# The last periods of a staged kernel get orders of their own, and key-value products move one more token tile behind their keys

## The chip, the core and the metric

The kernel runs on one core of a Trainium2 chip. The metric is the device time of one execution in microseconds (us), taken as the median of several executions.

## What is computed

The input is 4 sequences of 2048 tokens with 256 channels, in float32. Four residual layers follow one another, each as `x = x + norm(layer(norm(x)))` with a plain layer norm over the 256 channels:

1. softmax attention with 16 heads of 16 channels; queries and keys are the normalised input, scaled per channel, and values are the normalised input itself;
2. a feed-forward layer with token shift: `r = sigmoid(W_r xr)`, `k = relu(W_k xk)^2`, output `r * (W_v k)`, where `xr` and `xk` mix each token with the one before it;
3. a linear-attention block: norm, `Q = elu(q)+1`, `K = elu(k)+1`, the sums `KV = sum K v` over the tokens of a whole sequence, the message `Q KV / (Q sum K)`, then a second norm and a GELU layer of 1024 hidden channels;
4. a gated layer with integer weights: `W_d (silu(W_g x) * (W_u x))` with 768 hidden channels.

## The kernel before

**Two parts.** `sandwich_kernel` first does layer 1 for all four sequences and writes the result to DRAM (`mids`). Then `rest` does layers 2 to 4. This change touches `rest` alone. `rest` is built twice, and a flag computed from the integer weights picks one at run time; these inputs take the branch `narrow`, in which the hidden values of layer 4 are split into a high part `gT` and a low part `gL`.

**Blocks, stages, periods.** `rest` works on 16 blocks of 512 tokens (4 token tiles of 128), 4 blocks to a sequence. A block passes four stages, written as Python generators: `stage_f` (layer 2), `stage_a` (first norms, queries, keys and values of layer 3), `stage_b` (message and GELU layer of layer 3) and `stage_i` (layer 4). In period `p`, stage f works on block `p`, stage a on `p - 2`, stage b on `p - 6` and stage i on `p - 7`. So f runs in periods 0 to 15, a in 2 to 17, b in 6 to 21, i in 7 to 22, and what is left of i in 23. From period 18 on only b and i are left.

**Order.** The strings `RAMP` (periods 0 to 5) and `FULL` (6 to 23) list the parts of the stages in the order in which one period issues them; `next:` and `last:` take a part of the neighbouring period's block. A part whose block does not exist is skipped. TensorE (PE), ScalarE (ACT) and VectorE (DVE) are wrapped in `InOrder`, which keeps their instructions in exactly this order; all of them carry the helper's line, L46, so the profile's rows are told apart by tile names. GpSimd (POOL) and the SyncE queue (SP) are not wrapped: a scheduler places their instructions as their inputs and their buffers allow, and each then runs its own list in order.

**Parts that matter here.**

- `b:pre` (POOL, L537): `hb <- x`, the layer norm applied to the four token tiles of the block. `next:b.pre` stands behind `b:down3` in `FULL`, and `hb` has one buffer.
- `b:msg`: per token tile two products `m <- kvm,QT` on PE, three DVE steps that end in `msg`, and a POOL add `hb <- hb,msg` (L310). `b:sums` are DVE statistics (`lnb`), and the root is taken on POOL (L533). `b:norm` is four ACT steps `h <- hb` behind two small POOL steps (L117, L118). `b:turn` is eight PE transposes `t <- ident,h` with two ACT evacuations into `zT`.
- `b:up0` to `b:up3`: two of the eight hidden tiles each, `m <- zT,w1T` on PE and GELU on ACT. `b:down0` to `b:down3`: one token tile each, `m <- w2T,hf` on PE, a DVE add `o <- m,b` and a POOL add `o <- o,hb` (L332).
- `b:osums`, `b:x`: statistics `lno` on DVE, root `lno_rs` on POOL, four DVE steps `o <- o,lno_mv,lno_rs`, four POOL adds `x <- x,o` (L140). `i:osums` and `i:x` are the same for stage i, with the output's DMA at the end; the freed buffer then takes the next block's load (`load`, pool `late`).
- `i:sums`, `i:norm`, `i:turn`: the same pattern with `lni`. Each `i:turn` evacuation is an ACT copy `hT` and a DVE difference `hL`, both from the PSUM tile `t`, of which there are two.
- `i:gate0` to `i:gate5`: eight PE products, SiLU on ACT, `gs <- m,gs` on DVE, the copy `gT` on ACT, `gL <- gs,gT` on POOL (L382). `i:down0` to `i:down3`: twelve PE products each from `gT` and `gL`, and an ACT copy `o <- m`.
- `a:kv0` to `a:kv3`: per token tile `m <- wkv,zT` on PE; then `elu` on DVE, the exponential on ACT, `K` on DVE and `v` on ACT. `gather` adds `kv <- v,K` on PE, one token tile behind. `a:kv4` does the last gather.

All products of `rest` write PSUM tiles `m`, of which there are four.

Of the kernel before, what the change touches and what calls it, by code (L numbers as in the profile page):

```python
# [10 lines left out]
FP = mybir.dt.float32  # L11
# [7 lines left out]
P = 128  # L19
C = 256  # L20
CC = C // P
# [28 lines left out]
def rest(ctx: ExitStack, tc: tile.TileContext, a: dict, out_rows, mids, env: dict, narrow: bool):  # L50
    nc = tc.nc
# [16 lines left out]
    NB = B * NBLK  # L68
    LAG_A, LAG_B, LAG_I = 2, 2 + NBLK, 3 + NBLK
    early = ctx.enter_context(tc.tile_pool(name="early", bufs=3))  # L70
    late = ctx.enter_context(tc.tile_pool(name="late", bufs=3))
    quer = ctx.enter_context(tc.tile_pool(name="quer", bufs=LAG_B - LAG_A + 1))
    small = ctx.enter_context(tc.tile_pool(name="small", bufs=LAG_B - LAG_A + 2))
    one = ctx.enter_context(tc.tile_pool(name="one", bufs=1))
    two = ctx.enter_context(tc.tile_pool(name="two", bufs=2))
    three = ctx.enter_context(tc.tile_pool(name="three", bufs=3))
# [7 lines left out]
        dve.tensor_scalar(wq[name], wi, 1.0 if narrow else DEQUANT, None, ALU.mult)  # L84

    kvms, vs = [], []
    for r in range(2):
        kvm = one.tile([P, CC, P + 4], FP, tag=f"kvm{r}", name=f"kvm{r}")
        nc.gpsimd.memset(kvm, 0.0)
        kvms.append(kvm)  # L90

        v = one.tile([P, CC, P + 4], FP, tag=f"v{r}", name=f"v{r}")
        nc.gpsimd.memset(v, 1.0 / T)
        vs.append(v)
# [12 lines left out]
    def sums(src, tag, pool=two):  # L107
        return ln_stats(pool, [src[:, i, :] for i in range(4)], tag, dve)
# [110 lines left out]
    def stage_a(j):  # L219
        x, k = xs[j], j % NBLK  # L220
        before[j] = st = sums(x, "lna", small)
        yield "sums"
        h = block_tile("h")
        norm(h, x, st)
        st = sums(h, "lnz")
        yield "norm"
        norm(h, h, st)
        yield "norm2"
        zT = three.tile([P, CC, IB], FP, tag="zT", name="zT")
        to_channels(h, affine(zT, g1, be1))  # L230
        yield "turn"
        queries[j] = QT = quer.tile([P, CC, IB], FP, tag="QT", name="QT")
        for d in range(CC):
            qp = mm_tile()
            linear(qp, lambda c: wqT[:, c, d * P : (d + 1) * P], lambda c: zT[:, c, :], CC)
            elu1(QT[:, d, :], qp, IB)
            yield f"q{d}"
        if k == 0:
            kvacc[0] = [ps_kv.tile([P, P + 4], FP, tag=f"kv{c}", name=f"kv{c}") for c in range(CC)]
        kv = kvacc[0]  # L240

        def gather(i, K, V):
            for c in range(CC):
                pe.matmul(
                    kv[c],
                    lhsT=K[:, c * P : (c + 1) * P],
                    rhs=V[:, c, :],
                    start=(k == 0 and i == 0),
                    stop=(k == NBLK - 1 and i == 3),
                )  # L250

        last = None
        for i in range(4):
            kvp = mm_tile()
            linear(kvp, lambda c: zT[:, c, i * P : (i + 1) * P], lambda c: wkv[:, c, :], CC)
            K = two.tile([P, C], FP, tag="K", name="K")
            elu1(K, kvp[:, :C], C)
            V = vs[i % 2]
            act.activation(
                V[:, :, :P],  # L260
                kvp[:, C:].rearrange("p (c d) -> p c d", c=CC),
                AF.Copy,
                scale=1.0 / T,
            )
            if last:
                gather(*last)
            last = i, K, V
            yield f"kv{i}"
        gather(*last)
        if k == NBLK - 1:  # L270
            kvm = kvms[j // NBLK % 2]
            for c in range(CC):
                for g in range(4):
                    rows = slice(32 * g, 32 * g + 32)
                    dve.tensor_copy(kvm[rows, c, rows], kv[c][rows, rows])
                    dve.tensor_copy(
                        kvm[rows, c, P + g : P + g + 1], kv[c][rows, P + g : P + g + 1]
                    )
        yield "kv4"


    def stage_b(j):
        x, kvm, QT = xs[j], kvms[j // NBLK % 2], queries.pop(j)
        mv, rs = before.pop(j)
        hb = one.tile([P, 4, C], FP, tag="hb", name="hb")
        for i in range(4):
            ln_apply(hb[:, i, :], x[:, i, :], mv, rs, i, nc.gpsimd)
        yield "pre"
        for i in range(4):
            mp = mm_tile()  # L290
            m3 = mp[:, : CC * (P + 4)].rearrange("p (c k) -> p c k", c=CC)
            for c in range(CC):
                pe.matmul(
                    m3[:, c, :],
                    lhsT=QT[:, c, i * P : (i + 1) * P],
                    rhs=kvm[:, c, :],
                    start=True,
                    stop=True,
                )
            zr = two.tile([P, CC, 4], FP, tag="zr", name="zr")  # L300
            dve.tensor_scalar(zr, m3[:, :, P : P + 4], EPS_ATTN / T, None, ALU.add)
            dve.reciprocal(zr, zr)
            msg = three.tile([P, C], FP, tag="msg", name="msg")
            dve.tensor_tensor(
                msg.rearrange("p (c h v) -> p c h v", c=CC, h=4),
                m3[:, :, :P].rearrange("p c (h v) -> p c h v", h=4),
                zr.unsqueeze(3).broadcast_to([P, CC, 4, 32]),
                ALU.mult,
            )
            nc.gpsimd.tensor_tensor(hb[:, i, :], hb[:, i, :], msg, ALU.add)  # L310
        yield "msg"
        st = sums(hb, "lnb")
        yield "sums"
        z = block_tile("h")
        norm(z, hb, st)
        yield "norm"
        zT = three.tile([P, CC, IB], FP, tag="zT", name="zT")
        to_channels(z, affine(zT, g2, be2))
        yield "turn"
        hf = one.tile([P, NF, IB], FP, tag="hf", name="hf")  # L320
        for f in range(NF):
            fp = mm_tile()
            linear(fp, lambda c: w1T[:, c, f * P : (f + 1) * P], lambda c: zT[:, c, :], CC)
            act.activation(hf[:, f, :], fp, AF.Gelu, bias=b1[:, f : f + 1])
            if f % 2:
                yield f"up{f // 2}"
        o = block_tile("o")
        for i in range(4):
            yp = mm_tile()
            linear(yp[:, :C], lambda f: hf[:, f, i * P : (i + 1) * P], lambda f: w2T[:, f, :], NF)  # L330
            dve.tensor_tensor(o[:, i, :], yp[:, :C], b2, ALU.add)
            nc.gpsimd.tensor_tensor(o[:, i, :], o[:, i, :], hb[:, i, :], ALU.add)  # L332
            yield f"down{i}"
        st = sums(o, "lno")
        yield "osums"
        apply(o, o, st)
        residual(x, o)
        yield "x"


    def stage_i(j):
# [67 lines left out]
    FULL = (  # L409
        "f:turn i:turn b:msg i:gate0 a:turn last:i.osums f:mix i:gate1 b:sums last:i.x load i:gate2 f:k0 "  # L410
# [4 lines left out]
    )  # L415
    RAMP = (
        "load f:turn a:turn f:mix a:q0 next:a.sums a:q1 f:k0 next:a.norm f:k1 a:kv0 next:f.sums a:kv1 "
        "next:a.norm2 a:kv2 next:f.norm a:kv3 f:r a:kv4 f:v f:osums f:x next:b.pre"
    )
    MAKE = {"f": (stage_f, 0), "a": (stage_a, LAG_A), "b": (stage_b, LAG_B), "i": (stage_i, LAG_I)}  # L420
    live = {}

    def step(p, stage, part):
        make, lag = MAKE[stage]
        j = p - lag
# [10 lines left out]
    for p in range(NB + LAG_I + 1):  # L436
        if p < 3:
            convert(("wgT", "wuT", "wdT")[p])
        for item in (RAMP if p < LAG_B else FULL).split():
            if item == "load":  # L440
                if p + 1 < NB:
                    load(p + 1, early)
                if 0 <= p + 1 - LAG_B < NB:
                    load(p + 1 - LAG_B, late)
                continue
            stage, part = item.split(":")
            at = p
            if stage in ("next", "last"):
                at = p + 1 if stage == "next" else p - 1
                stage, part = part.split(".")  # L450
            step(at, stage, part)
# [517 lines left out]
```

## Time and profile before

| | us |
|---|---|
| median of 3 runs | 4577.19 (4576.31 to 4578.02) |
| the profiled execution | 4576.01 |
| span of its instructions | 4574.2 |
| layer 1 (attention) | to about 3087 |
| periods 0 to 5 (`RAMP`) | to 3321 |
| periods 6 to 17 | 3321 to 4272.5 |
| periods 18 to 23 (b and i only) | 4272.5 to 4574.2 |

Period starts are read from the first transposes of `i:turn` (or `f:turn`) in the timeline. A row of the timeline has the start, the duration of all its instructions from first start to last end, the engine, the line, the operation, the tiles, the shape, the number of instructions, and in brackets the idle time before it and what ended it. A row of the windows has the stretch, its length, each engine's busy time with its instructions, the clock that TensorE was granted as a share of full speed, and the DMA share and rate. A row of the waits names the waiting engine and tile, what it waited for, the total, the number and the longest.

### The profile page before, as it was taken

The page shows a single profiled execution, that of the slowest core. Times are in us where ns is not written, and L with a number is a line of the kernel's source. Part 1 is how long each engine was busy: PE and PEld are TensorE (multiplying, and loading weights), DVE is VectorE, ACT ScalarE, POOL GpSimd, SP SyncE. Part 2 cuts the span into 40 slices and gives each one's busy share as a digit, 9 for nine tenths or more (in the row PEclk, how much of TensorE's full clock was granted, in tenths as well). Part 3 has the DMA queues.
Part 4 walks back from the last instruction along what each step waited for, and adds up shares of the span by engine and source line. Part 5 has one row for each costly group of instructions (what it writes and reads, how often), then busy time and mean ns, then how long its engine had stood idle before and what let it go on. Part 6 is the DMA issues. An engine that isn't in the chain of part 4 may idle for free.

```text
span 4574.2 us, 69494 instructions
## 1 busy us (share of the span) xinstructions
PE 4196.7 (92%) x26369; PEld 2196.9 (48%) x26369; DVE 3394.8 (74%) x6847; ACT 2874.5 (63%) x3558; POOL 1089.5 (24%) x1541
## 2 busy tenths in 40 slices
PE   4999999999999999999999999984789899899887
PEld 1444444444444444444444444432456666666665
DVE  4898898988889988889898888954555545554333
ACT  0677777777777777777777777763555555655343
POOL 3100111211001221011121100013234544444344
PEclk9999999999999999999999999997999999999998
DMA  3101101011010020110101101002000000000000
GB/s 107 38 10 29 29 10 42 29 43 36 11 30 23 25 65 10 29 29 10 43 29 31 38 10 29 1 24 72 33 14 28 19 33 24 28 19 19 10 19 15
DMA packets 84568, 130.58 MB, mean 29 GB/s; under 512 B 21376, under 2 KB 41984, under 8 KB 84224
## 3 DMA queue, kind: packets, MB, share of 16 engines
q1 hardware_dynamic: 77920, 122.23, 9.0%
q8 instruction: 210, 3.44, 0.3%
q10 hardware_dynamic: 6304, 3.81, 0.3%
q14 instruction: 134, 1.10, 0.1%
HBM read 33.70 MB, written 25.17 MB: 13 GB/s over the span
## 4 chain that ended last, share of the span: by engine, by line
PE 60%; DVE 21%; ACT 9%; POOL 5%; issue 4%; SPq 1%; DMA 1%; ACTq 0%; POOLq 0%; DVEq 0%
PE acc L46 19%; PE s L46 17%; PE w L46 13%; DVE mx L46 10%; PE m L46 8%; PE t L46 2%; ACT p L46 2%; DVE o L46 2%; ACT h L46 2%; POOL hb L537 2%; ACT L46 1%; DVE gs L46 1%; SPq L662 1%; ACT elu L46 1%; PE ot L46 1%
## 5 line engine op out<-in xcount | busy, mean ns | idle before, releaser
L46 DVE TENSOR_REDUCE mx<-s 128x1 f32<-128x512 f32 x4096 | 2538.8, 682 | 305.0 <-PE s L46 304.9
L46 ACT ACTIVATE p<-w 128x1024 f32<-128x1024 f32 x2048 | 2002.7, 1022 | 824.4 <-PE s L46 556.9
L46 PE MATMUL s<-k,q 64*128 64x512 f32 x4096 | 1664.3, 450 | 56.8 <-DMA k<-lo 30.3
L46 PE MATMUL w<-mrow,pick 64*128 64x512 f32 x4096 | 1406.2, 417 | 0.0
L46 PE MATMUL w<-q,k 64*128 64x512 f32 x4096 | 1369.3, 419 | 0.0
L46 PEld LDWEIGHTS s<-k,q 64*128 64x128 f32 x4096 | 758.5, 186 | 1269.2 <-DVE mx L46 1147.0
L46 PE MATMUL acc<-p,xp 128*32 128x512 f32 x8192 | 1093.3, 605 | 0.0
L46 PEld LDWEIGHTS w<-mrow,pick 64*128 64x128 f32 x4096 | 749.1, 185 | 55.2
L46 PEld LDWEIGHTS w<-q,k 64*128 64x128 f32 x4096 | 670.5, 185 | 58.2 <-ACT p L46 21.7
L627 POOL TENSOR_SCALAR xd<-x,lnx_nm,lnx_rs 128x128 f32<-128x128 f32 x256 | 110.9, 448 | 991.3 <-PE t L46 991.0
L609 POOL TENSOR_SCALAR xp<-x,lnx_nm,lnx_rs 128x64 f32<-128x64 f32 x256 | 99.1, 394 | 921.9 <-PE acc L46 921.0
L46 PEld LDWEIGHTS acc<-p,xp 128*32 128x32 f32 x8192 | 161.6, 108 | 247.0 <-issue 245.8
L46 DVE SCALAR_TENSOR_TENSOR gs<-m,gs 128x512 f32<-128x512 f32 x96 | 66.2, 690 | 226.9 <-ACT gs L46 205.6
L46 PE MATMUL m<-zT,w1T 128*128 128x512 f32 x512 | 225.4, 593 | 0.4 <-ACT zT L46 0.4
L46 PE MATMUL m<-w2T,hf 128*128 128x256 f32 x1024 | 225.6, 379 | 0.0
L46 PEld LDWEIGHTS m<-w2T,hf 128*128 128x128 f32 x1024 | 194.6, 190 | 38.4 <-issue 13.4
L382 POOL TENSOR_TENSOR gL<-gs,gT 128x512 fp32r<-128x512 f32 x96 | 124.4, 1296 | 198.3 <-ACT gT L46 198.2
L46 PE MATMUL t<-ident,h 128*128 128x128 f32 x512 | 90.2, 312 | 88.5 <-ACT h L46 55.9
L46 ACT ACTIVATE elu<-elu 128x256 f32<-128x256 f32 (+1 forms) x96 | 46.7, 487 | 196.4 <-DVE elu L46 196.2
L46 ACT ACT_TABLE_LOAD x102 | 130.9, 1283 | 58.3 <-DVE elu L46 24.6
L46 PEld LDWEIGHTS m<-zT,w1T 128*128 128x128 f32 x512 | 97.4, 190 | 110.6 <-issue 99.3
L140 POOL TENSOR_TENSOR x<-x,o 128x256 f32<-128x256 f32 x192 | 141.8, 767 | 17.9 <-DVE o L46 17.9
(146 smaller groups left out, 4065.4 us busy)
## 6 DMA issues: line engine op xcount, KB each, us to landing
q<-hi SPq DMA_DIRECT2D x256, 64.0 KB, 2.1
k<-hi SPq DMA_DIRECT2D x256, 64.0 KB, 2.1
q<-lo SPq DMA_DIRECT2D x256, 64.0 KB, 2.1
k<-lo SPq DMA_DIRECT2D x256, 64.0 KB, 2.1
mid<-x SPq DMA_DIRECT2D x32, 512.0 KB, 2.6
x<-mid SPq DMA_DIRECT2D x32, 512.0 KB, 3.3
x<-in_x SPq DMA_DIRECT2D x16, 512.0 KB, 5.8
out<-x SPq DMA_DIRECT2D x16, 512.0 KB, 2.9
```

The source lines that it names most:

```text
L46: return lambda *args, **kw: self._tc.keep_in_program_order(method(*args, **kw))
L140: nc.gpsimd.tensor_tensor(x[:, i, :], x[:, i, :], o[:, i, :], ALU.add)
L382: nc.gpsimd.tensor_tensor(gL[:, f, :], gs, gT.bitcast(FP)[:, f, :], ALU.subtract)
L537: dve.tensor_scalar(dst, src, mv[:, i, 0:1], rs[:, i : i + 1], ALU.subtract, ALU.mult)
L609: nc.gpsimd.tensor_scalar(heads(n)[:, i, :, :HD], xs[b][:, i, g * GH * HD : (g + 1) * GH * HD].rearrange("p (h d) -> p h d", d=HD), nm[:, ...
L627: nc.gpsimd.tensor_scalar(xd[:, i], xh.unsqueeze(1).broadcast_to([P, 2, GH * HD]), nm[:, it : it + 1], rs[:, it : it + 1], ALU.add, ALU.mult,)
L662: nc.sync.dma_start(out=dst.bitcast(FP)[r::4, cols], in_=part.bitcast(FP)[c0 : c0 + 32, :])
```

## The change

Three edits, all in `rest`.

- **Two orders for the end.** Period 18 runs `TURN`, periods 19 to 23 run `LATE`. In both, the gates and downs of stage i come behind the ups and downs of stage b; `next:b.msg` moves up into the gates, and the statistics, norms and transposes of the next block's two stages stand among `i:down0` to `i:down3`. In `LATE` the period begins with what is left of the last block of stage i and with `b:turn`.
- **Gathers two tiles behind.** `gather` runs two token tiles behind the keys, everywhere; `K` gets three buffers, and the constant-padded values `v` three.
- **Buffers.** `hb` has two instead of one, `msg` two instead of three, `QT` four instead of five.

Since POOL's list is made by the scheduler, the second `hb` buffer also moves `hb <- x`: in periods 7 to 17 it stands in front of `gL` of gates 4 and 5, where it stood between the last `o <- o,hb` and the root `lno_rs` of `b:osums`. The second block's `hb <- x` is done in period 3, where one instruction of it stands between the two small steps `nb` of `a:norm` and three ahead of the squares `ka`. SP's list is the same.

```diff
-    quer = ctx.enter_context(tc.tile_pool(name="quer", bufs=LAG_B - LAG_A + 1))
+    quer = ctx.enter_context(tc.tile_pool(name="quer", bufs=LAG_B - LAG_A))
...
-        last = None
+        behind = []
         for i in range(4):
...
-            K = two.tile([P, C], FP, tag="K", name="K")
+            K = three.tile([P, C], FP, tag="K", name="K")
             elu1(K, kvp[:, :C], C)
-            V = vs[i % 2]
+            V = vs[i % 3]
...
-            if last:
-                gather(*last)
-            last = i, K, V
+            behind.append((i, K, V))
+            if i > 1:
+                gather(*behind.pop(0))
             yield f"kv{i}"
-        gather(*last)
+        for late in behind:
+            gather(*late)
...
-        hb = one.tile([P, 4, C], FP, tag="hb", name="hb")
+        hb = two.tile([P, 4, C], FP, tag="hb", name="hb")
...
-            msg = three.tile([P, C], FP, tag="msg", name="msg")
+            msg = two.tile([P, C], FP, tag="msg", name="msg")
...
+    TURN = (
+        "i:turn b:msg i:gate0 last:i.osums b:sums i:gate1 last:i.x load b:norm i:gate2 "
+        "b:turn b:up0 next:b.pre b:up1 b:up2 b:up3 b:down0 b:down1 b:down2 b:down3 b:osums i:gate3 "
+        "i:gate4 b:x i:gate5 next:b.msg i:down0 next:i.sums next:b.sums i:down1 "
+        "next:i.norm i:down2 next:b.norm i:down3 next:i.turn"
+    )
+    LATE = (
+        "last:i.osums b:turn b:up0 last:i.x load b:up1 b:up2 next:b.pre b:up3 b:down0 b:down1 b:down2 "
+        "b:down3 b:osums i:gate0 i:gate1 b:x i:gate2 i:gate3 i:gate4 next:b.msg i:gate5 next:i.sums "
+        "i:down0 next:b.sums i:down1 next:i.norm i:down2 next:b.norm i:down3 next:i.turn"
+    )
...
-        for item in (RAMP if p < LAG_B else FULL).split():
+        order = LATE if p > NB + LAG_A else TURN if p == NB + LAG_A else FULL if p >= LAG_B else RAMP
+        for item in order.split():
```

More of the change, by code (lines that the diff above doesn't have):

```diff
@@ L86, in rest @@
     kvms, vs = [], []
[L87 to L90, printed above, removed]
+    for r in range(3):
+        if r < 2:
+            kvm = one.tile([P, CC, P + 4], FP, tag=f"kvm{r}", name=f"kvm{r}")
+            nc.gpsimd.memset(kvm, 0.0)
+            kvms.append(kvm)
         v = one.tile([P, CC, P + 4], FP, tag=f"v{r}", name=f"v{r}")
```

## The prediction

> **What bounds the kernel now.** I read the page first, then the windows by period, then PE's waits, then the timelines of all engines around each wait.
>
> ```profile
> PE   4999999999999999999999999984789899899887
> PEclk9999999999999999999999999997999999999998
> ```
>
> PE is full until the switch to the second part and loses tenths there and at the end. Layer 1, untouched, keeps its 3087 us. The windows of a middle period and of periods 18, 19 and 21:
>
> ```profile
> 3476.95:3558.80 81.85, 74.61 (x320) 51.61 (x321) 42.84 (x130) 46.25 (x80) 39.61 (x50) 1.00 0.08 26
> 4272.51:4339.13 66.62, 53.59 (x224) 39.81 (x225) 23.83 (x83) 25.52 (x41) 29.32 (x34) 0.87 0.05 16
> 4339.13:4406.64 67.51, 54.57 (x225) 39.63 (x225) 21.99 (x68) 25.59 (x41) 29.31 (x34) 0.88 0.05 16
> 4472.99:4537.39 64.40, 54.78 (x224) 40.41 (x224) 22.02 (x68) 25.57 (x41) 24.50 (x30) 0.90 0.03 9
> ```
>
> A middle period has PE at work 74.6 of 81.9 us at full clock. A late period has it at work 54 of 67, and at a lower clock. PE's waits from 4272.5 to the end are nearly one kind, two a period:
>
> ```profile
> PE t L46 <- ACT h L46: 48.1, 12, 8.6
> ```
> ```profile
> 3556.66 1.04 PE L46 MATMUL t<-ident,h 128*128 128x128 f32 x8
> 4146.70 0.33 PE L46 MATMUL t<-ident,h 128*128 128x128 f32 x1 [2.97 <-ACT h L46]
> 4472.99 2.80 PE L46 MATMUL t<-ident,h 128*128 128x128 f32 x8 [8.58 <-ACT h L46]
> 4491.38 2.80 PE L46 MATMUL t<-ident,h 128*128 128x128 f32 x8 [4.17 <-ACT h L46]
> ```
>
> Transposes wait for a norm: `i:turn` 8.6 us, `b:turn` 4.2 us. Eight transposes then take 2.80 us instead of 1.04, so each wait is also paid in clock, for 3 to 7 us afterwards.
>
> **The ends of the middle periods.** Here a chain, not PE, sets when gather 3 and the transposes can start:
>
> ```profile
> 3542.59 4.85 POOL L537 TENSOR_SCALAR hb<-x,lna_mv,lna_rs 128x256 f32<-128x256 f32 x4
> 3547.41 1.04 POOL L533 TENSOR_TENSOR lno_rs<-lno_ve,neghalf 128x4 f32<-128x4 f32 x1
> ```
> ```profile
> 3548.48 2.22 DVE L46 TENSOR_SCALAR o<-o,lno_mv,lno_rs 128x256 f32<-128x256 f32 x4 [1.40 <-POOL lno_rs L533]
> 3550.62 0.41 DVE L46 TENSOR_SCALAR elu<-m 128x256 f32<-128x256 f32 x1
> ```
> ```profile
> 3556.10 0.72 PE L46 MATMUL kv<-v,K 128*128 128x132 f32 x4 [1.45 <-ACT v L46]
> 3558.80 1.14 PE L46 MATMUL t<-ident,h 128*128 128x128 f32 x8 [1.11 <-ACT hT L46]
> ```
>
> `lno_ve` is ready at 3545.8, but POOL works on `hb <- x` until 3547.4. DVE's four `o` steps wait 1.40 us for the root, `elu` of token tile 2 stands behind them, and from `v` of tile 2 (3552.1) ACT hardly rests up to the copies `hT` at 3558.2. Moving gathers alone changes nothing: `v` of tile 3 still comes out of ACT at 3556.05, and PE waits there whatever it has done before. Moving `hb <- x` pays: the root runs at 3545.9, the `o` steps follow `K` of tile 1 at 3547.1, 1.4 us earlier, and `elu` of tile 2 at 3549.2 still finds its product, done by 3548.7. ACT's run moves up 1.4 us, `hT` and the second transposes with it. PE, which gains 0.6 us from the gather moved out of its way, waits about 0.65 us at gather 3 instead of 1.45; next late is ACT's run itself. In its new place `hb <- x` falls into a POOL gap (idle 5.4 us before 3588.2; its block's load is issued at 3581.2 and a load takes 3.3). Gate 4's `gL` slips from 3588.2 to about 3589.5, and the next need, `lno_rs` of `f:osums`, is at 3597.5. Period 17 waits only 0.4 us for its root. Sum: 10 x 1.4 + 0.4 = **14.4 us**; bounds 0 (another ACT step late) and 11 x 1.7 = 19.
>
> **The ramp.** PE's gathers wait 21 us in periods 0 to 6, and none of it comes back. Each ramp period ends so:
>
> ```profile
> 3272.45 2.06 ACT L46 ACTIVATE h<-x,nb,lnf_rs 128x256 f32<-128x256 f32 x4
> 3274.41 0.41 ACT L46 ACTIVATE elu<-elu 128x256 f32<-128x256 f32 x1
> ...
> 3277.06 1.21 ACT L46 ACTIVATE r<-m 128x256 f32<-128x256 f32 x4
> ```
>
> Norms, exponentials, `v`, a table load and the sigmoids stand in one ACT line, and `f:v` waits for the last of them. A PE that comes earlier to `f:v` waits longer there. In period 3, one `hb <- x` (1.22 us) between the two `nb` steps delays a norm at the head of that line: **-1.4 us** (bounds 0 and -5, all four). Three `K`, `v` and four `QT` buffers cost nothing: gather and `b:msg` read the old contents before they are needed again. Two `msg` buffers cost 0.1 us or less in a middle period, where POOL adds as DVE produces.
>
> **A late period.** PE's own work is 2.3 (16 transposes at 1.15 for 8) + 14.0 (up: 32 products, of which 24 took 10.46) + 14.0 (down: 13.98) + 11.2 (gates, 48 at 0.233) + 2.9 (message) + 5.6 (down of i, 48 at 0.117) = 50.0 us. The question is what of the norm chains the new order covers. I set T to PE's end of `b:down3` and follow the queues with these rows:
>
> ```profile
> 4542.47 1.28 ACT L46 ACT_TABLE_LOAD   x1 [1.65 <-PE m L46]
> ```
> ```profile
> 4548.58 2.80 DVE L46 TENSOR_SCALAR o<-o,lno_mv,lno_rs 128x256 f32<-128x256 f32 x4 [0.55 <-POOL lno_rs L533]
> ...
> 4553.16 0.69 DVE L46 SCALAR_TENSOR_TENSOR gs<-m,gs 128x512 f32<-128x512 f32 x1 [1.18 <-ACT gs L46]
> 4555.04 0.69 DVE L46 SCALAR_TENSOR_TENSOR gs<-m,gs 128x512 f32<-128x512 f32 x1 [1.18 <-ACT gs L46]
> ```
>
> - One gate takes 1.88 us on the ring copy, SiLU, `gs`, as long as on PE. The first SiLU waits for a table load, so `gs` of gate 0 runs at T+3.15 and of gate 1 at T+5.0. `b:x` adds its 2.8 us on DVE: gate 2 at T+8.4, gate 4 at T+12.2.
> - `m` tiles come free with these steps, so `next:b.msg` ends on PE near T+13.6. Its DVE steps start at T+12.9 and take 0.77 each; POOL is still at `gL` of gate 4 until T+14.9, adds at 0.74, and with two `msg` buffers the fourth `msg` ends at T+16.85 (with three, 0.8 earlier).
> - Behind it on DVE: `gs` of gate 5, `next:i.sums` (2.4, to T+19.95), `next:b.sums` (2.25, to T+22.2). From the last statistics step to ACT's norm the trace has 1.75 us (4470.59 to 4472.34). So ACT does i's norm T+21.7 to 23.75, a copy `o`, b's norm T+24.15 to 26.2, another `o`, the first `hT` to T+27.15; DVE's `hL` frees the PSUM tile at T+27.9. Then `b:turn`, the first `zT` (0.72), and `b:up0` starts at **T+29.5**.
> - With up and down: 29.5 + 28.0 = 57.5 us. PE has two gaps on the way, 2.3 us (for `gL` of gate 5) and 2.8 us (for the `t` tile).
>
> The clock: the 2.97 us gap before 4146.70 was followed by transposes at 0.24 each, where 0.12 is normal, so gaps of this size can halve the clock. I add 2.5 us per late period, between 0 and 5: **60.0 us**, against 67.5 and 66.4 now. Bounds for the period are 50 (PE alone) and 65 (both waits as long as today's, less the second clock loss).
>
> The Trainium skill ("TensorE: Matmul & The Clock Gate", section "What's actually happening") says that the clock halves after about one idle window of 3.4 us. The trace agrees for the 8.58 and 4.17 us gaps, but not for the one of 2.97 us; by the rule the late periods would keep full clock, the third rival below.
>
> **Period 18 and the end.** S is 4272.51. `TURN` puts `b:sums` ahead of gate 1's `gs`, so `b:turn` starts 1.5 us earlier, at S+15.6. With a slow restart up begins at S+18.4 and T is S+47.5. Then three gates, where the same bookkeeping gives up at T+25.7, and with 2 us of clock the next T at S+103.2. Two periods of 60 follow, T at S+223. Without a next message `i:turn` of the last block starts 21.2 us later, S+244.4; today it is S+264.9 (4537.39). From there to the last `gs` today takes 19.5 us at a slow clock, afterwards 17.3: the last block's `i:osums` and `i:x` now stand ahead of gate 0 on DVE, but PE restarts warm. The 17.3 us behind are unchanged. Sum of the end: 20.5 + 2.2 = **22.7 us**; bounds 5 and 40.
>
> `hb <- x` in `LATE` waits on POOL for a load that follows the output's DMA. I get the load landed by T+42 and `hb <- x` done by T+47, ahead of the four `o <- o,hb` (the last at T+58).
>
> **Sum.** 14.4 - 1.4 + 22.7 = 35.7 us off the profiled 4576.0 is 4540.3. The median of the runs is 1.2 above the profiled time: **4541 us**. A difference under 0.2% (9 us) can't be told from none.
>
> **The rivals.**
>
> - *The middle gains nothing* (chance 0.15). ACT's run before `hT` could be late for another reason, for example the norm of i, whose statistics wait for POOL's `x` adds. Against it: these adds start with the `o` steps, so they move up too. Then only the end pays: 4541 + 14 = 4555.
> - *The late chain is longer than my bookkeeping* (0.09). i's and b's norms run in one line through DVE, POOL, ACT and the two `t` tiles; if up starts at T+35, a late period takes 65 us and the end gains some 5: 4559. With the rival above as well: 4573, no change that can be told (0.03).
> - *The clock stays up in the short gaps* (0.12). For it: gaps of 1.45 and 1.11 us in the middle cost none. Against: the 2.97 us row. It saves 3 x 2.5 + 2 = 9.5: 4531.
> - *Slower: POOL stands behind a load* (0.04). `hb <- x` now heads POOL's queue while its load may be on the way, once a period from 8 to 17. From a landing at 3584.5 the work in front of `lno_rs` leaves 5.5 us to 3597.5, and DVE rests another 5.9 us before the `elu` behind it. The load takes 3.3 us in the median, so it would have to land 11.4 us late. Every us beyond costs a period 1 us; with the 13 of the middle lost, the end's 22.7 is used up from 2.3 us beyond, and 4 us beyond give 4541 + 13 + 40 = 4594.
>
> **How the numbers follow.** My forecast has 0.57, its own range 4531 to 4552 (late period 57 to 63, middle 10 to 17). Going to the first rival and the clock rival, and halfway to the long chain: 4524 to 4560 for 8 in 10. Faster by over 0.2%: 0.57 + 0.15 + 0.09 + 0.12 = 0.93; same 0.03; slower 0.04.
>
> **What would show it.** Right: middle periods of 80.4 us with DVE's `o` steps no longer waiting for `lno_rs`; ramp periods unchanged at 38.8 although `kv` waits are gone; late periods near 60 with `PE t <- DVE hL` or `ACT hT` instead of `ACT h`, and a stall for `gL` in `i:down0`; half the table loads. Wrong: middle periods of 81.8; late periods under 55 or over 64; a POOL wait for `x <- mid`.

## The result and the profile after

The changed kernel takes 4556.39 us (median of 6 runs, 4554.78 to 4558.44) against 4578.16 us (6 runs, 4576.31 to 4579.18) for the kernel before: a ratio of 0.9953 (95% interval 0.994 to 0.9966), some 22 us faster. The forecast was 4541, with 4524 to 4560 as its range. So about 15 us of the forecast gain are missing. The profiled executions have spans of 4574.2 and 4554.4 us; all accounts below are made between spans.

The page of the kernel after, the busy tenths of PE and its clock:

```profile
PE   4999999999999999999999999985779989999887
PEclk9999999999999999999999999997989999999999
```

At this grain the two pages hardly differ; the gain at the end has to be read in the windows, where the clock from period 18's message on is 0.94 on average, against 0.88 before. The windows of a middle period, of the period behind the switch and of the late period after it:

```profile
3566.70:3648.10 81.40, 74.32 (x323) 51.72 (x321) 44.93 (x146) 46.31 (x80) 39.63 (x50) 1.00 0.08 26
4331.40:4390.90 59.50, 52.30 (x217) 36.92 (x215) 24.72 (x72) 21.72 (x36) 29.73 (x37) 0.91 0.05 18
4390.90:4449.10 58.20, 52.34 (x226) 37.33 (x225) 23.39 (x69) 22.64 (x38) 29.32 (x35) 0.97 0.06 19
```

A late period has fallen from 66 or 67 us to 58 or 59, close to the forecast 60. A middle period has gone from 81.85 to 81.4, not to the forecast 80.4. PE's waits from 4272 us to the end, of the kernel after, confirm that the pattern at the end has changed: the 48.1 us that stood behind `ACT h` have become 7.8, and the waits for `hL` and `gL` that the bookkeeping had are there.

```profile
PE t L46 <- ACT h L46: 7.8, 6, 5.1
PE t L46 <- DVE hL L46: 7.4, 3, 2.5
PE m L46 <- POOL gL L384: 6.0, 7, 1.0
```

I split every span at two marks, the first message product `m <- kvm,QT` of block 0 (start of period 6) and of block 12 (in period 18). Ramp, middle and end then compare as follows; the lower rows are the experiments of the next section, in the same measure.

| kernel | to block 0's message | twelve periods | the end | span |
|---|---|---|---|---|
| before | 3320.8 | 953.8 | 299.6 | 4574.2 |
| after | 3328.4 | 950.3 | 275.7 | 4554.4 |
| gathers one behind again | 3322.8 | 938.4 | 275.7 | 4536.9 |
| tiny copy ahead of the SiLU | 3326.2 | 940.3 | 276.3 | 4542.8 |
| one behind, three `v` | 3322.4 | 949.0 | 275.4 | 4546.8 |
| before with two `hb` | 3321.5 | 938.2 | 290.6 | 4550.3 |
| orders with one `hb` | 3323.3 | 953.9 | 284.8 | 4562.0 |
| before with the gather edit | 3328.3 | 967.0 | 303.7 | 4599.0 |
| tiny copy, gathers behind `f:v` | 3331.0 | 941.4 | 275.1 | 4547.5 |
| one behind, three `msg` | 3322.5 | 938.1 | 272.4 | 4533.0 |

After against before: the ramp loses 7.6, the middle gains 3.5, the end gains 23.9; together 19.8.

**The middle.** The end of a period improved just as forecast. POOL's root and DVE's `o` steps, kernel after:

```profile
3554.20 1.04 POOL L548 TENSOR_TENSOR lno_rs<-lno_ve,neghalf 128x4 f32<-128x4 f32 x1 [3.34 <-DVE lno_ve L46]
...
3592.42 4.86 POOL L552 TENSOR_SCALAR hb<-x,lna_mv,lna_rs 128x256 f32<-128x256 f32 x4 [1.79 <-DMA x<-mid]
```
```profile
3555.34 2.21 DVE L46 TENSOR_SCALAR o<-o,lno_mv,lno_rs 128x256 f32<-128x256 f32 x4
```

The root runs as soon as `lno_ve` is there, and the `o` steps carry no wait. What was won is lost a few us later, at gate 0. First ACT before, then ACT after:

```profile
3559.49 1.07 ACT L46 CAST hT<-t 128x512 fp32r<-128x512 f32 x2 [0.26 <-PE t L46]
3560.59 1.28 ACT L46 ACT_TABLE_LOAD   x1
3563.53 0.60 ACT L46 ACTIVATE gs<-m 128x512 f32<-128x512 f32 x1 [1.66 <-PE m L46]
```
```profile
3566.40 1.07 ACT L46 CAST hT<-t 128x512 fp32r<-128x512 f32 x2 [0.26 <-PE t L46]
3570.47 1.28 ACT L46 ACT_TABLE_LOAD   x1 [2.99 <-PE m L46]
3571.76 0.60 ACT L46 ACTIVATE gs<-m 128x512 f32<-128x512 f32 x1
```

Before, the table load for SiLU ran right behind `hT`, while PE was still at the gate's products, and cost nothing. After, the load itself stands still for 2.99 us until PE's product is done, and only then loads: SiLU is 1.28 us late. PE meets that at the first `xk` product. PE before, then PE after:

```profile
3570.20 1.98 PE L46 MATMUL m<-xk,WkT 128*128 128x512 f32 x4 [1.17 <-ACT gs L46]
```
```profile
3578.07 1.98 PE L46 MATMUL m<-xk,WkT 128*128 128x512 f32 x4 [2.15 <-ACT gs L46]
```

That is 0.98 us in each period. The clock is not the reason: the window above, of a period of 81.40 us, has it at 1.00. In the built programs the reason can be read. Before, the SiLU of gate 0 waits for one semaphore (a counter on which instructions wait), PE's, and the wait is its own. After, it needs PE's and ACT's own; the wait for PE has become an instruction by itself, and that stands ahead of the table load. (In the last four blocks of the kernel before it is so already: the load at 4542.47 waits for PE.)

**The ramp.** The end of a ramp period on PE, before and then after:

```profile
3235.24 3.62 PE L46 MATMUL m<-WrT,xr 128*128 128x256 f32 x16
3238.70 0.61 PE L46 MATMUL kv<-v,K 128*128 128x132 f32 x4
3239.16 3.69 PE L46 MATMUL m<-WvT,ka 128*128 128x256 f32 x16
3242.69 1.04 PE L46 MATMUL t<-ident,h 128*128 128x128 f32 x8
```
```profile
3238.27 1.13 PE L46 MATMUL m<-WrT,xr 128*128 128x256 f32 x4 [0.76 <-ACT v L46]
3241.48 1.50 PE L46 MATMUL m<-WrT,xr 128*128 128x256 f32 x4 [2.07 <-ACT v L46]
3242.77 1.97 PE L46 MATMUL kv<-v,K 128*128 128x132 f32 x8
3244.53 4.11 PE L46 MATMUL m<-WvT,ka 128*128 128x256 f32 x16
3248.47 1.04 PE L46 MATMUL t<-ident,h 128*128 128x128 f32 x8
```

Before, PE came through `f:r`, one gather and `f:v` without a pause. After, it waits inside `f:r` for the `m` tiles of key tiles 2 and 3, because the gathers that used to wait there have moved away, and then both last gathers stand in front of `f:v`. They take 1.97 us and `f:v` 4.11: behind the waits the granted clock is 0.50, from 3242.1 to 3245.5. The kernel before has half clock in this period too, from 3223.3 to 3233.4, but there it is over 5 us before ACT's `r`, which `f:v` needs, and costs nothing that can be seen. From ACT's first `r` (3238.63 before, 3242.74 after) to the transposes it is 4.06 us before and 5.73 after, so 1.67 more; a ramp period goes from 38.4 to 40.1.

### The profile page after: what moved, and what is told of

It is laid out like the page before. It is cut to its first block, busy times and chain, and to the rows that moved or that the text cites. A ratio compares the mean times of both kernels' runs of the same rounds, so it can differ in the third digit from the quotient of the medians.

```text
span 4554.4 us, 69526 instructions
## 1 busy us (share of the span) xinstructions
PE 4198.6 (92%) x26369; PEld 2196.8 (48%) x26369; DVE 3397.4 (75%) x6847; ACT 2865.5 (63%) x3550; POOL 1092.2 (24%) x1542
## 4 chain that ended last, share of the span: by engine, by line
PE 65%; DVE 19%; ACT 9%; issue 4%; POOL 2%; SPq 1%; DMA 1%; ACTq 0%; DVEq 0%; POOLq 0%
PE acc L46 19%; PE s L46 17%; PE m L46 13%; PE w L46 13%; DVE mx L46 10%; PE t L46 2%; ACT p L46 2%; ACT h L46 2%; ACT L46 1%; DVE gs L46 1%; DVE o L46 1%; ACT gs L46 1%; DVE lno_st L46 1%; ACT zT L46 1%; SPq L677 1%
## 5 line engine op out<-in xcount | busy, mean ns | idle before, releaser
L46 PEld LDWEIGHTS m<-w2T,hf 128*128 128x128 f32 x1024 | 194.6, 190 | 38.4 <-issue 13.4
L46 ACT ACT_TABLE_LOAD x94 | 120.6, 1283 | 137.8 <-PE m L46 92.7
L46 ACT ACTIVATE hf<-m,b 128x512 f32<-128x512 f32 x128 | 86.8, 687 | 109.8 <-PE m L46 109.5
```

The lines of the kernel that those rows point to most:

```text
L46: return lambda *args, **kw: self._tc.keep_in_program_order(method(*args, **kw))
```

## The experiments

The ratios are to 4576.72 us, the median of ten runs of the kernel before that were taken with these. Every kernel here has four `QT` buffers.

**The gather edit undone.** All else stays as in the kernel after.

```diff
-            K = three.tile([P, C], FP, tag="K", name="K")
+            K = two.tile([P, C], FP, tag="K", name="K")
...
-            V = vs[i % 3]
+            V = vs[i % 2]
...
-            behind.append((i, K, V))
-            if i > 1:
-                gather(*behind.pop(0))
+            if last:
+                gather(*last)
+            last = i, K, V
...
```

> The changed kernel with its gathers one token tile behind again (K and v two buffers each); the two orders for the end and the hb, msg and QT buffers stay. Theory A, the gather edit is what ate the missing gain: a third v buffer makes ACT's table load ahead of gate 0's SiLU wait for PE's product (about 1.0 us in each of some 10 middle periods), and gathers 2 and 3 standing between f:r and f:v stretch the ramp periods from 38.8 to 40.5 us (5.6 us over periods 3 to 6). Undoing it then gives about 4540 us, middle periods of 80.4 and ramp periods of 38.8. Theory B, the loss comes from hb <- x in its new place on POOL or from two msg buffers: nothing changes, 4556, middle periods of 81.4.

Measured: 4539.06 us (4537.91 to 4541.39), ratio to before 0.9919 (0.9905 to 0.9932). Middle periods are 80.4, the end is 275.7 as in the kernel after, and the last three full ramp periods, counted from the first `xk` product to the next, are 39.3, 38.4 and 38.8 (before 38.8, 38.4 and 38.8; after 41.0, 40.1 and 40.6). Theory B falls: with `hb <- x` in its new place and two `msg` buffers, the whole middle gain is there as soon as the gathers are back. ACT at gate 0 of this kernel:

```profile
3559.51 1.28 ACT L46 ACT_TABLE_LOAD   x1
```

The load waits for nothing again.

**Only the table load freed.** Gathers stay two behind, `K` and `v` stay three. One column of the last norm is copied ahead of gate 0's SiLU, which makes ACT wait for its own earlier work in an instruction of its own.

```diff
...
+            if narrow and f == 0:
+                act.copy(seen, h[:, 3, :1])
             act.activation(gs, gp, AF.Silu, scale=scale)
```

> The changed kernel with one tiny ACT copy (128x1, out of the last norm of stage i) ahead of gate 0's SiLU, so that the SiLU has a single wait again and the table load in front of it has none; gathers two behind and three v buffers stay. Theory A: the load runs right behind hT again, each middle period becomes about 1.0 us shorter (80.4) less some 0.1 to 0.2 us for the copy, the ramp keeps its 40.5: about 4547 us. Theory B (the load's wait is hidden, the later SiLU is due to something else in front of gate 0): middle periods stay at 81.4, 4556 us, or a little above.

Measured: 4546.79 us (4544.96 to 4547.41), ratio 0.9934 (0.992 to 0.9947). Middle periods are 80.4, though an instruction was added. ACT's timeline:

```profile
3563.30 0.20 ACT L46 COPY seen<-h 128x1 f32<-128x1 f32 x1
3563.51 1.28 ACT L46 ACT_TABLE_LOAD   x1
3566.36 0.60 ACT L46 ACTIVATE gs<-m 128x512 f32<-128x512 f32 x1 [1.57 <-PE m L46]
```

So the load's wait is the loss in the middle: the copy wins back 10.0 of the 11.9 us by which the kernel after and the one with the gathers undone differ there. The copy's 0.20 us lie in ACT's idle time. And since 80.4 comes with gathers one or two behind, the second tile of lag earns nothing there.

**Only the third `v` buffer.** Gathers one behind, `K` two, `v` three.

```diff
-            K = three.tile([P, C], FP, tag="K", name="K")
+            K = two.tile([P, C], FP, tag="K", name="K")
...
-            if i > 1:
+            if i > 0:
                 gather(*behind.pop(0))
```

> The changed kernel with gathers one token tile behind and two K buffers, but with the three v buffers kept: it differs from the kernel with the gather edit undone in the third v buffer alone. Theory A: the ramp is back at 38.8 us a period (the gathers' place made it longer), while the middle stays at about 81.4 (the third buffer makes the table load wait): about 4549 us. Rival: the gathers' place alone does all of it, then 4540, as with the whole edit undone.

Measured: 4549.28 us (4548.65 to 4552.53), ratio 0.9941 (0.9928 to 0.9955): the ramp is back at 39.3, 38.4 and 38.8, the middle periods stay at 81.4. The two costs come apart: the lag (with the third `K` that comes with it) makes the ramp longer, the buffer of `v` makes the load wait. Alone it costs 10.6 us in the twelve periods (949.0 against 938.4). ACT's row:

```profile
3564.17 1.28 ACT L46 ACT_TABLE_LOAD   x1 [2.99 <-PE m L46]
```

How a buffer of `v` puts a wait on a SiLU is only argued, not shown: with two buffers ACT's `v` depends on a younger gather, and through PE's progress ACT's own earlier steps count as done; with three it depends on an older one, so the SiLU has to ask for itself.

**Only the second `hb` buffer**, in the kernel before (with three `msg`).

```diff
-        hb = one.tile([P, 4, C], FP, tag="hb", name="hb")
+        hb = two.tile([P, 4, C], FP, tag="hb", name="hb")
```

> The kernel before with two hb and four QT buffers and nothing else: hb <- x moves on POOL, gathers and orders are the old ones. Theory A, by the prediction's middle term: middle periods of 80.4 instead of 81.9, 14.4 us off in all, 1.4 lost in period 3: about 4565 us. Rival (the chain behind lno_rs is not what bounds the end of a middle period): 81.8 us a period, 4577.

Measured: 4553.97 us (4552.07 to 4554.47), ratio 0.9949 (0.9936 to 0.9963), 11 us better than the theory. The middle is as forecast, 80.4 a period and 15.6 in all. The surprise is the end: 9.0 us less in the old order too, with late periods of 62.5, 64.4 and 64.7 instead of 67.1, 67.5 and 66.4. POOL in a late period, before and then with two `hb`:

```profile
4393.82 4.85 POOL L537 TENSOR_SCALAR hb<-x,lna_mv,lna_rs 128x256 f32<-128x256 f32 x4
4398.64 1.03 POOL L533 TENSOR_TENSOR lno_rs<-lno_ve,neghalf 128x4 f32<-128x4 f32 x1
```
```profile
4375.92 1.04 POOL L533 TENSOR_TENSOR lno_rs<-lno_ve,neghalf 128x4 f32<-128x4 f32 x1 [1.60 <-DVE lno_ve L46]
```

Before, `lno_ve` was done at 4395.24 and its root began 3.40 us later, behind `hb <- x`; that is the collision of the middle periods (1.62 us there), twice as large. The late periods became 4.6, 3.1 and 1.6 us shorter.

**The orders with one `hb` buffer**, gathers one behind, two `msg`. One buffer is still read until `b:down3`, so `next:b.pre` moves behind it in both orders.

```diff
-        "last:i.osums b:turn b:up0 last:i.x load b:up1 b:up2 next:b.pre b:up3 b:down0 b:down1 b:down2 "
-        "b:down3 b:osums i:gate0 i:gate1 ...
+        "last:i.osums b:turn b:up0 last:i.x load b:up1 b:up2 b:up3 b:down0 b:down1 b:down2 "
+        "b:down3 next:b.pre b:osums i:gate0 i:gate1 ...
...
```

> The two orders for the end without the second hb buffer: gathers one behind, hb one buffer, and next:b.pre moved behind b:down3 in both orders (as in FULL), since one buffer is still read until then. With only the second hb buffer the old order already lost 9 of the 24 us at the end, as POOL's hb <- x no longer stood in front of the root lno_rs. Theory: the orders by themselves give some 15 us. hb <- x delays lno_rs by about 3.4 us here, of which some 2.3 reach DVE's o steps behind gate 1, so a late period takes about 60.5 us instead of 58.2 and the middle stays at 81.9: about 4562 us. Rival 1: the orders cover that delay (o steps have room), late periods of 58.2, the full 24: 4553. Rival 2: without the early hb the message of the next block comes late too and the orders gain nothing: 4577.

Measured: 4563.2 us (4562.28 to 4564.13), ratio 0.9969 (0.9957 to 0.9981). The orders (with two `msg`) give 14.8 us at the end; with the 9.0 of the buffer that makes 23.8, where the kernel after has 23.9. The two late periods, 65.9 and 61.9 us, are longer than the 60.5 expected. From block 12's message to block 13's, in period 18, it takes 52.0 us, where the kernel after has 52.7. POOL and PE show the price of the one buffer:

```profile
4382.93 4.86 POOL L550 TENSOR_SCALAR hb<-x,lna_mv,lna_rs 128x256 f32<-128x256 f32 x4
4387.75 1.03 POOL L546 TENSOR_TENSOR lno_rs<-lno_ve,neghalf 128x4 f32<-128x4 f32 x1
```
```profile
4393.23 0.80 PE L46 MATMUL m<-hT,wuT 128*128 128x512 f32 x1 [3.29 <-DVE gs L46]
```

The gate behind `b:x` waits 3.29 us for DVE, where the kernel after has 0.48 in this place.

**Only the gather edit**, in the kernel before.

> The kernel before with the gather edit (two tiles behind, three K and three v buffers) and four QT buffers, and nothing else. Theory A: this edit alone makes the kernel slower: ramp +5.6 us, and in the middle the table load of gate 0 waits for PE: between +0.5 and +1.0 us in each of some 11 periods: 4587 to 4594 us. Rival: in the old kernel PE's wait at gather 3 (1.45 us) is freed by it and pays for the table load: 4577 to 4583.

Measured: 4598.58 us (4595.6 to 4600.9), ratio 1.0045 (1.0031 to 1.0058): slower, by 22 us, and some 5 us above theory A's upper end. Ramp +7.5, twelve periods +13.2 (82.9 or 83.5 each), end +4.1. The rival falls: nothing pays for the load. I had not counted the clock. PE of this kernel:

```profile
3580.44 3.51 PE L46 MATMUL m<-xk,WkT 128*128 128x512 f32 x4 [2.15 <-ACT gs L46]
...
3648.29 0.72 PE L46 MATMUL kv<-v,K 128*128 128x132 f32 x4 [1.97 <-ACT v L46]
3648.84 1.74 PE L46 MATMUL t<-ident,h 128*128 128x128 f32 x8
```

Gather 3 now waits 1.97 us instead of 1.45, the eight transposes behind it take 1.74 instead of 1.04, and `xk` after gate 0's wait takes 3.51 instead of 1.98. The granted clock is 0.50 at both places (3649.1 to 3652.4, and 3580.8 to 3584.1). At the end, where no gather is left, the clock is 0.86 on average, against 0.88 before; why it is lower there stays open.

**What in the ramp costs the time.** The tiny copy stays in, and the last two gathers go behind `f:v`.

```diff
-        "next:a.norm2 a:kv2 next:f.norm a:kv3 f:r a:kv4 f:v f:osums f:x next:b.pre"
+        "next:a.norm2 a:kv2 next:f.norm a:kv3 f:r f:v a:kv4 f:osums f:x next:b.pre"
```

> The changed kernel with the tiny ACT copy ahead of gate 0's SiLU, and in RAMP a:kv4 (the last two gathers) moved behind f:v. It tells what in the ramp costs 1.7 us a period. If the gathers that stand between f:r and f:v cost only their own 0.5 us and PE's low clock comes from its waits for m tiles in f:r, ramp periods go from 40.5 to 40.0: 4545. If the low clock in f:v goes away too, they go back to 38.8: 4541. If the m tiles alone set it, nothing changes: 4547.

Measured: 4549.58 us (4547.39 to 4550.02), ratio 0.9938 (0.9925 to 0.9952), 3 us worse than with the copy alone and above all three times expected. The first two of the three ramp periods are 40.3 and 40.0 us, where the copy alone has 41.0 and 40.1, so the gathers' place is worth 0.7 and 0.1 us. PE's timeline:

```profile
3240.80 1.13 PE L46 MATMUL m<-WrT,xr 128*128 128x256 f32 x4 [2.07 <-ACT v L46]
3242.59 5.24 PE L46 MATMUL m<-WvT,ka 128*128 128x256 f32 x16 [0.66 <-ACT r L46]
3247.66 1.06 PE L46 MATMUL kv<-v,K 128*128 128x132 f32 x8
...
3342.73 6.34 PE L46 MATMUL m<-xk,WkT 128*128 128x512 f32 x8 [7.87 <-DVE xk L46]
```

`f:v` now starts right behind ACT's `r` (3242.06), but the granted clock is 0.50 from 3242.3 to 3245.7, so `f:v` takes 5.24 us instead of 3.69, and the gathers come on top, in front of the transposes. So the half clock goes with PE's pauses (0.76, 2.07, 0.66), which lie just ahead of `f:v`, and not with the gathers' place; no run changes the pauses alone. The two intervals behind these take 86.8 us together, where the copy alone has 81.7; the long wait for `xk` lies in the second.

**Three `msg` buffers**, gathers one behind.

```diff
-            msg = two.tile([P, C], FP, tag="msg", name="msg")
+            msg = three.tile([P, C], FP, tag="msg", name="msg")
```

> The changed kernel with the gather edit undone and three msg buffers instead of two. The prediction's bookkeeping has the fourth msg end 0.8 us earlier with three buffers in a late period: 4539 less about 3 (4 periods of 0.8) gives 4536. Rival: b's norm is not what the late period's end waits for: 4539, late periods stay at 58.2.

Measured: 4534.61 us (4533.63 to 4537.51), ratio 0.9908 (0.9893 to 0.9924): 4.5 us less than with two buffers, the end 3.3 shorter, late periods 57.7 and 57.4, which is 2.0 and 0.9 us less. The total is the one expected, but not as four times 0.8. The third `msg` on DVE, kernel after and then with three buffers:

```profile
4396.23 0.43 DVE L46 TENSOR_TENSOR msg<-m,zr 128x256 f32<-128x256 f32 x1 [0.92 <-POOL hb L312]
```
```profile
4375.13 0.42 DVE L46 TENSOR_TENSOR msg<-m,zr 128x256 f32<-128x256 f32 x1
```

The 0.92 us wait for POOL's add is gone. This version beats both kernels: the new orders and two `hb`, without the gather edit and with three `msg`.

## Why the prediction was right or wrong

The measured 4556 us lie inside the range of 4524 to 4560, but outside the forecast's own 4531 to 4552, and that they lie inside is partly luck. Of the three terms only the end's held. The middle fell short by 10.9 us and the ramp by 6.2, for reasons that no rival names (the middle's lower bound says no more than "another ACT step late"). The range took them in because it reached to a rival with another cause.

- **The end** (22.7 forecast, 23.9 measured) was right in size and in its steps. With T at 4380.55, the start of gate 0, DVE's `gs` of gate 0 runs at T+3.3 (3.15 forecast), DVE's fourth `msg` ends at T+16.9 (16.85), and `b:up0` starts at 4409.64, T+29.1 (29.5). PE's gaps of 2.47 us for `hL` and 2.03 for `gT` and `gL` are those of the bookkeeping (2.8 and 2.3). Table loads fell from four to two a late period, as said. PE in the late period after:

```profile
4349.40 1.97 PE L46 MATMUL t<-ident,h 128*128 128x128 f32 x8 [2.48 <-DVE hL L46]
...
4398.80 0.39 PE L46 MATMUL m<-wdT,gT 128*128 128x256 f32 x1 [1.06 <-ACT gT L46]
4400.15 0.39 PE L46 MATMUL m<-wdT,gL 128*128 128x256 f32 x1 [0.97 <-POOL gL L384]
4408.11 1.25 PE L46 MATMUL t<-ident,h 128*128 128x128 f32 x8 [2.47 <-DVE hL L46]
```

  The clock allowance of 2.5 us a period was too large: periods of 59.5 and 58.2 against 57.5 leave 2.0 and 0.7. The last term was smaller than said: from the last `i:turn` to the end it takes 36.3 us (from 4518.05) where it took 36.8, a gain of 0.5 and not 2.2. What the prediction did not see is whose gain it was: 9 of the 24 us come from the second `hb` buffer, which gives them in the old order as well.
- **The middle** (14.4 forecast, 3.5 measured): that the `o` steps start 1.4 us earlier and ACT's run moves up with them is what the runs showed, 15.6 us with two `hb` alone. The failed step is "Three `K`, `v` and four `QT` buffers cost nothing": the third `v` costs 0.98 us a period at gate 0, 10.6 of the 11.9 us that the whole gather edit takes in the middle. It was weighed by who reads the buffers, not by which waits the built program then carries, and so not by what stands in front of the instruction that gets one.
- **The ramp** (-1.4 forecast, -7.6 measured, outside its bounds): `hb <- x` cost 0.5 and not 1.4, seen as 39.3 instead of 38.8 in the first of the three ramp periods of each kernel with two `hb` and gathers one behind. Some 5.2 belong to the gathers, three periods of 1.7 or 1.8. The step that failed is "A PE that comes earlier to `f:v` waits longer there", which put the moved waits at no cost: they are not at `f:v` but inside `f:r`, and behind them stand two gathers and half clock, on the way to the end of the period. The other 2 us lie at the very start and can't come from the order: from the first `xk` product to that of the next period it takes 25.4 us with the tiny copy and 27.5 in the kernel after, with the same ramp instructions in the same order. They are the clock: from 3126.1 to 3129.4 it is 1.00 with the tiny copy and 0.50 in the kernel after, and `f:v` takes 3.69 us with the one and 5.17 with the other; the `xk` products ahead of it take 5.34 and 6.29. Why the stretches of half clock lie at other times there is open.
- **The rivals.** "The middle gains nothing" names a time, 4555, close to the measured one, but not the cause: ACT's run before `hT` was not late. "POOL stands behind a load" has its wait, 1.79 us for `x <- mid`, which the prediction named as a sign of being wrong, and it is harmless: `lno_rs` of `f:osums` runs 37.7 us behind the period's first message product in the kernel before and also in the one with gathers one behind. The long late chain did not come. Full clock in the late periods came in part.

The Trainium skill ("ScalarE: Activation LUTs", section "What ACT_TABLE_LOAD costs") gives a switch of tables about 1283 ns for the load and about 1380 ns more for a drain. The load's 1.28 us agree; the drain does not show. In the kernel before the load starts 0.03 us after the copies `hT` end, in the kernel after the SiLU starts 1.29 us after the load does, and the period grew by 1.0 us.

Not tried: four `QT` buffers alone. Open: why the gather edit costs the old order 4.1 us at the end.

## What to carry to other kernels

A buffer added "for nothing" can change which waits the built program needs. Look at the instruction that follows a table load: here, once it had to wait for two things, the load waited too, and a load that was free became part of the chain. Before an order is credited with a gain, run the buffers that come with it alone; and wait time that an edit takes from PE is only won if PE then has work that is ready, otherwise it turns up again just ahead of the bound work.

## What the hardware showed that I had not expected

PE's clock falls after shorter pauses than I had thought: one wait of 1.97 us in a middle period (gathers edit alone) was followed by transposes at 1.74 us for eight instead of 1.04, and one of 2.48 us in a late period by 1.97, while another of 2.47 us gave 1.25. Waits of 1.45 and 1.11 us in the kernel before cost nothing, nor did the 2.15 us ahead of `xk` in the middle period of the kernel after, while a wait of the same 2.15 us was followed by half clock with the gather edit alone. So the length of a pause does not decide by itself; what else does is not shown. The Trainium skill ("TensorE: Matmul & The Clock Gate", section "What's actually happening") puts the fall behind an idle window of about 3.4 us; the row of 1.97 us disagrees, and the measurement decides.
